# Transposing attention weights in 32x32 squares on VectorE, with a detour through DRAM, in a two-layer graph kernel

**Chip, cores, metric.** One Trainium2 chip, one core. Times are device microseconds (us) of one execution, median over runs.

## The reference

128 graphs of 128 nodes with 512 features pass through two layers. Each adds a graph operation to x and normalizes the sum. All data are fp32.

```python
def _L0_gnn_ref(x, adj, Wq, Wk, Wv):
    q = jnp.einsum('bnd,ed->bne', x, Wq); k = ...; v = ...
    rel = adj.T[None] * jnp.einsum('bnd,bmd->bnm', q, k)
    rel = rel / jnp.linalg.norm(rel, axis=2, keepdims=True)
    return jnp.einsum('bnm,bmd->bnd', rel, v)

def _L1_gnn_ref(x, adj, Wq, bq, Wk, bk, Wv, bv):        # 8 heads of 64
    q = (x @ Wq + bq).reshape(b, n, 8, 64); k = ...; v = ...
    scores = jnp.einsum('bihd,bjhd->bhij', q, k) / 8 + mask(adj)
    weights = jax.nn.softmax(scores, axis=-1)
    return jnp.einsum('bhij,bjhd->bihd', weights, v).reshape(b, n, 512)

x = _layernorm(x + _L0_gnn_ref(x, adj, ...))
x = _layernorm(x + _L1_gnn_ref(x, adj, ...))
```

## The kernel before

The 128 graphs are worked in 32 groups of four, here called batches 0 to 3. A group needs five projections of 512x512 (`m` and `v0` for layer 0; `q`, `k`, `v1` for layer 1). Each is made of seven half-sized products, in Strassen's manner, which share two PSUM banks "a" and "b" and a third, "d". Each product is 8 matmuls and takes 1.73 us from start to start.

A hand-written schedule runs in rounds of 35 slots. `dense` puts one product into a slot; `short` hangs the rest on slots, in the order in which each engine then works it off. Slot `7*j + k` belongs to projection j, so slot 21 holds the first product of the `k` projection.

```python
R = 35
for r in range(-1, NG):
    todo = [("m", r + 1), ("v0", r + 1), ("q", r), ("k", r), ("v1", r)]
    for j, (kind, g) in enumerate(todo):
        ...
        for k, i in ((0, 1), (2, 5), (3, 2), (4, 6), (5, 3), (6, 7), (8, 4)):   # slot, product
            dense[R * r + 7 * j + k] = (pr, i)
# ... layer 0, of the next group:
for b in range(G):
    at(g - 1, 10 + b, l0_score, g, b)
    at(g - 1, 18 + 2 * b, l0_out, g, b)
# ... layer 1:
    s = 31 + 5 * b
    at(g, s, attn_scores, g, b)
    at(g, s + 1, attn_max, g, b)
    at(g, s + 2, attn_exp, g, b, 0, 0)
    # ... three more pairs of exponentials
    at(g, s + 4, attn_transpose, g, b, 0)
    at(g, s + 6, attn_transpose, g, b, 1)
    at(g, s + 7, attn_out, g, b)
    at(g, s + 9, attn_stats, g, b)
    at(g, s + 11, attn_store, g, b)
```

The softmax weights are transposed by TensorE, four heads a block, and a copy brings each block from PSUM to SBUF:

```python
def attn_transpose(g, b, s):
    w, wT = SOFT[g, b][0], SOFT[g, b][3]
    wT[s] = two.tile([P, H // 2, P], F32, tag="wT", ..., bufs=3)
    p = ps_m.tile([P, H // 2, P], F32, tag="m", ...)
    for a in range(H // 2):
        nc.tensor.transpose(p[:, a, :], w[:, s, a, :], ident)
    if s: nc.scalar.copy(wT[s], p)
    else: nc.vector.tensor_copy(wT[s], p)

def attn_out(g, b):
    # ...
    for h in range(H):
        nc.tensor.matmul(p[:, h, :], wT[h % 2][:, h // 2, :], V1[g][:, b, h * HD:(h + 1) * HD], ...)
```

The layer-1 input x1 is already transposed on VectorE in 32x32 squares. DMAs inside SBUF first bring the squares to their places, 16 for each half of a group:

```python
def x1_stage(g, h):
    t = stage(g, h, "h")
    for q in range(A):
        for a in range(A):
            nc.sync.dma_start(t[q*Q:(q+1)*Q, :, a, :], X[g, h][a*Q:(a+1)*Q, :, q*P:(q+1)*P])
```

## Time and profile before

| | before |
|---|---|
| time, median of 4 runs beside the kernel after | 2782.45 us (2779.79 to 2782.64) |
| span of the profiled run, mean granted TensorE clock | 2778.2 us, 0.990 |
| busy TensorE / VectorE / ScalarE | 98% / 59% / 30% of the span |
| all DMA traffic, packet share of the queue | 143.6 MB, 19.4% |
| TensorE's waits on VectorE's copies of the weights | 3.5 us in the whole span |

TensorE is busy throughout and waits almost only at the start, so a round costs what TensorE's own instructions cost. In the profiled run I mark each round by the start of the first product of the `k` projection, slot 21 in both kernels. There are 32 marks: the first at 128.58 us, then 30 rounds of 84.15 us each, then a last round of 62.56 us (it has no `m` and `v0` work), then 62.6 us to the end.

### The profile page before, as it was taken

Reading aid. Unit: us, or ns where it says so; the run is one execution under the profiler, and the core shown is the slowest. Engines: PE = TensorE matmul, PEld = TensorE weight load, DVE = VectorE, ACT = ScalarE, POOL = GpSimd, SP = SyncE. Lnnn points to the kernel's source line nnn. Section 1 sums busy time; section 2 is a strip of 40 time slices with the busy share of each in tenths; the row PEclk is TensorE's granted clock in tenths of the full one; section 3 lists DMA queues with packets and bytes.
Section 4 is the critical chain, followed back from the end, with each engine's and each line's share of the span. In section 5 each row is a group of like instructions: output and inputs, shape, how many; then the busy total and the mean of one; then the engine's idle time right before and its main releaser. Section 6 shows DMA issues by size and latency. Waiting matters only on the chain. (4 is left out here: it accounts for less than half of the span.)

```text
span 2778.2 us, 41137 instructions
## 1 busy us (share of the span) xinstructions
PE 2726.0 (98%) x15648; PEld 2353.6 (85%) x15648; DVE 1643.9 (59%) x2709; ACT 835.5 (30%) x2951; POOL 609.5 (22%) x763
## 2 busy tenths in 40 slices
PE   7799999999999999999999999999999999999998
PEld 5688888888888888888888888888888888888877
DVE  4356656656556556566566566566566565565664
ACT  1133222332223333223333223332233322233332
POOL 4111122222122222122121222121222221222211
PEclk9899999999999999999999999999999999999998
DMA  6121121221221220222221222211212202212110
GB/s 141 46 58 43 41 57 51 57 58 29 52 58 51 56 58 27 58 55 53 58 52 33 57 53 55 58 39 45 56 51 58 58 25 56 57 51 57 42 34 21
DMA packets 193831, 143.57 MB, mean 52 GB/s; under 512 B 24928, under 2 KB 158176, under 8 KB 193632
## 3 DMA queue, kind: packets, MB, share of 16 engines
q1 hardware_dynamic: 193632, 140.94, 19.4%
q8 instruction: 123, 2.02, 0.3%
q14 instruction: 76, 0.62, 0.1%
HBM read 73.73 MB, written 33.55 MB: 39 GB/s over the span
## 5 line engine op out<-in xcount | busy, mean ns | idle before, releaser
L420 POOL TENSOR_TENSOR o<-o,x 128x512 f32<-128x512 f32 x128 | 162.2, 1267 | 1418.6 <-DVE o L418 1418.6
L394 ACT ACTIVATE w<-w,nmax 128x128 f32<-128x128 f32 x1024 | 398.8, 393 | 197.3 <-DVE nmax L388 195.7
L267 PE MATMUL pa_v<-wc_v,tx 128*128 128x256 f32 x1536 | 366.5, 381 | 0.8 <-DVE v L285 0.8
L267 PEld LDWEIGHTS pa_v<-wc_v,tx 128*128 128x128 f32 x1536 | 281.9, 190 | 38.2 <-DVE v L285 1.2
L415 PEld LDWEIGHTS po<-v,wT 128*128 128x128 f32 x2048 | 252.0, 194 | 13.0 <-DVE wT L406 4.3
L415 PE MATMUL po<-v,wT 128*128 128x64 f32 x2048 | 247.0, 274 | 5.4 <-DVE wT L406 3.5
L379 DVE SCALAR_TENSOR_TENSOR w<-ps,mask 128x1024 f32<-128x1024 f32 x128 | 156.7, 1224 | 89.3 <-PE ps L376 89.2
L267 PE MATMUL pa_m<-tx,wc_m 128*128 128x256 f32 x768 | 188.2, 388 | 21.3 <-DVE yT L285 19.1
L267 PEld LDWEIGHTS pa_q<-tx,wc_q 128*128 128x128 f32 x768 | 145.8, 190 | 59.5 <-issue 37.8
L394 ACT ACTIVATION_READ_ACCUMULATOR w<-w,nmax 128x1 f32 x1024 | 194.8, 190 | 0.0
L267 PE MATMUL pa_q<-tx,wc_q 128*128 128x256 f32 x768 | 181.5, 379 | 0.0
L267 PE MATMUL pa_k<-tx,wc_k 128*128 128x256 f32 x768 | 181.4, 379 | 0.0
L267 PEld LDWEIGHTS pa_m<-tx,wc_m 128*128 128x128 f32 x768 | 142.1, 191 | 42.7 <-issue 19.4
L418 DVE TENSOR_TENSOR o<-po,rs 128x512 f32<-128x512 f32 x128 | 88.5, 692 | 146.2 <-PE po L415 145.9
L281 ACT ACTIVATE s_q<-pa_q,bq_sb 128x256 f32<-128x256 f32 x128 | 53.6, 470 | 370.2 <-PE pa_q L267 370.2
L402 PE MATMUL pwT<-ident,w 128*128 128x128 f32 x1024 | 159.2, 277 | 4.3 <-ACT w L394 4.0
L267 PEld LDWEIGHTS pa_k<-tx,wc_k 128*128 128x128 f32 x768 | 145.9, 190 | 19.8
L376 PEld LDWEIGHTS ps<-kT,qT 64*128 64x128 f32 x2048 | 125.9, 189 | 41.5 <-issue 40.9
L402 PEld LDWEIGHTS pwT<-ident,w 128*128 128x128 f32 x1024 | 129.7, 143 | 33.1 <-ACT w L394 7.4
L388 DVE TENSOR_REDUCE nmax<-w 128x8 f32<-128x1024 f32 x128 | 154.9, 1210 | 0.0
L376 PE MATMUL ps<-kT,qT 64*128 64x128 f32 x2048 | 150.6, 287 | 0.0
L322 PE MATMUL pst<-yT,xT 128*128 128x128 f32 x1024 | 139.9, 280 | 0.0
(142 smaller groups left out, 4733.2 us busy)
## 6 DMA issues: line engine op xcount, KB each, us to landing
xl_x<-in_x_dram SPq DMA_DIRECT2D x256, 128.0 KB, 5.0
x<-in_x_dram SPq DMA_DIRECT2D x64, 512.0 KB, 5.1
xl_h<-x SPq DMA_DIRECT2D x1024, 32.0 KB, 1.9
out_dram<-o SPq DMA_DIRECT2D x128, 256.0 KB, 2.0
wv_s<-in_L_gnn_Wv_dram SPq DMA_DIRECT2D x8, 256.0 KB, 8.1
wq_s<-in_L_gnn_Wq_dram SPq DMA_DIRECT2D x1, 1024.0 KB, 5.6
wk_s<-in_L_gnn_Wk_dram SPq DMA_DIRECT2D x1, 1024.0 KB, 8.4
wq_s<-in_L_gnn_Wq_dram SPq DMA_DIRECT2D x4, 256.0 KB, 9.0
```

The source lines that it names most:

```text
L267: nc.tensor.matmul(bank[:, m, :], l[:, k, m * P:(m + 1) * P], r[:, k, :], start=start and m == 0 and k == 0, stop=(m == 1 and k == 1), ski ...
L281: nc.scalar.activation(dst[:, m], bank[:, m], AF.Identity, bias=b1[k][:, 2 * eh + m:2 * eh + m + 1])
L322: nc.tensor.matmul(p, XT[g][:, dc, b, :], YT[g][:, dc, b, :], start=(dc == 0), stop=(dc == C - 1))
L376: nc.tensor.matmul(p[:, s, a, :], QT[g][r, a, b, :], KT[g][r, a, b, :], start=True, stop=True)
L379: nc.vector.scalar_tensor_tensor(wf, p.rearrange("p s a j -> p (s a) j"), HD ** -0.5, mask[:, None, :].to_broadcast([P, H, P]), op0=ALU.mu ...
L388: nc.vector.tensor_reduce(nmax, w.rearrange("p s a j -> p (s a) j"), axis=AX.X, op=ALU.max, negate=True)
L394: nc.scalar.activation(w[:, s, a, :], w[:, s, a, :], AF.Exp, bias=nmax[:, i:i + 1], accum_out=sums[:, h:h + 1])
L402: nc.tensor.transpose(p[:, a, :], w[:, s, a, :], ident)
L415: nc.tensor.matmul(p[:, h, :], wT[h % 2][:, h // 2, :], V1[g][:, b, h * HD:(h + 1) * HD], start=True, stop=True)
L418: nc.vector.tensor_tensor(o.rearrange("p (h e) -> p h e", h=H), p, rs[:, :, None].to_broadcast([P, H, HD]), op=ALU.mult)
L420: nc.gpsimd.tensor_tensor(o, o, graph(g, b), op=ALU.add)
```

## The change

The intent is to take the 256 transpose blocks and their copies off the kernel's busiest engine. VectorE transposes only inside 32x32 squares, so the weights are written to DRAM and read back with the squares in their places. Then one VectorE instruction transposes all eight heads. x1 takes the same kind of detour in place of the 32 small copies of a group. The order of products gives VectorE more time before bank "a" is written again. `attn_out` moves from step s + 7 to s + 11. Layouts of scores, mask and maximum follow (the maximum becomes two instructions, the mask four), and the output tile `o` has two buffers in place of three.

```diff
+    def x1_spill(g, h):
+        X1D[g, h] = dram.tile([2, P, D], F32, tag="x1d", name=f"x1d_{g}_{h}")
+        nc.sync.dma_start(X1D[g, h].rearrange("b n d -> n b d"), X[g, h])
     def x1_stage(g, h):
-        t = stage(g, h, "h")
-        for q in range(A):
-            for a in range(A):
-                nc.sync.dma_start(t[q * Q:(q + 1) * Q, :, a, :], X[g, h][a * Q:(a + 1) * Q, :, q * P:(q + 1) * P])
+        load_staged(g, h, X1D.pop((g, h)))
 # ... (scores, mask, maximum and exponentials in the new layout: cut)
-    def attn_transpose(g, b, s):
-        # ... TensorE transposes and two copies, as above
+    def attn_spill(g, b, s):
+        if s == 0:
+            WD[g, b] = dram.tile([P, A, 2, H // 2 * Q], F32, tag="wd", name=f"wd_{g}_{b}")
+        nc.sync.dma_start(WD[g, b][:, :, s], SOFT[g, b][0][:, s].rearrange("p q a r -> p q (a r)"))
+    def attn_stage(g, b):
+        wl = one.tile([P, A, H, Q], F32, tag="wl", name=f"wl_{g}_{b}")
+        SOFT[g, b][0] = wl
+        rows = WD.pop((g, b)).rearrange("(a s) q t f -> s a q (t f)", s=Q)
+        for q in range(A):
+            nc.sync.dma_start(wl[q * Q:(q + 1) * Q].rearrange("p a i r -> p a (i r)"), rows[:, :, q, :])
+    def attn_transpose(g, b):
+        wT = one.tile([P, H, A, Q], F32, tag="wT", name=f"wT_{g}_{b}")
+        nc.vector.transpose(wT, SOFT[g, b][0].rearrange("p a i r -> p i a r"))
+        SOFT[g, b][0] = wT
 # ...
-            for k, i in ((0, 1), (2, 5), (3, 2), (4, 6), (5, 3), (6, 7), (8, 4)):
+            for k, i in ((0, 1), (1, 5), (3, 6), (4, 2), (5, 3), (6, 7), (9, 4)):
 # ...
-            at(g, s + 4, attn_transpose, g, b, 0)
-            at(g, s + 6, attn_transpose, g, b, 1)
-            at(g, s + 7, attn_out, g, b)
-            at(g, s + 9, attn_stats, g, b)
-            at(g, s + 11, attn_store, g, b)
+            at(g, s + 4, attn_spill, g, b, 0)
+            at(g, s + 6, attn_spill, g, b, 1)
+            at(g, s + 7, attn_stage, g, b)
+            at(g, s + 10, attn_transpose, g, b)
+            at(g, s + 11, attn_out, g, b)
+            at(g, s + 13, attn_stats, g, b)
+            at(g, s + 15, attn_store, g, b)
```

## The prediction

> **What bounds the kernel now.** I read the engine shares of the page first, then the waits of TensorE alone, then the timeline of TensorE in one steady round, then the timelines of VectorE and of the DMA queue, and last the DMA issues. The engine shares and the first waits:
>
> ```profile
> PE 2726.0 (98%) x15648; PEld 2353.6 (85%) x15648; DVE 1643.9 (59%) x2709; ACT 835.5 (30%) x2951; POOL 609.5 (22%) x763
> ...
> PE pa_m L267 <- DVE yT L285: 19.1, 1, 19.1
> PE pM L162 <- DMA wk_s<-in_L_gnn_Wk_dram: 9.7, 1, 9.7
> PE pwT L402 <- ACT w L394: 4.0, 2, 2.7
> ```
>
> TensorE works almost throughout, and all its waits together are 44 us. The longest, 19.1 us, happens once, near 79 us into the span. So a steady round costs what TensorE's instructions cost, and the other engines (DVE 59%) have room. A round of four batches takes about 84.7 us. I get this from the scores of the first batch of a group, which start at 1409.91 us and, 16 rounds later, at 2733.00 us; the last round lacks two of the five projections and the layer-0 work, some 32 us, so (1323.1 + 32) / 16 = 84.7. The cost of the transposes is read from the timeline of TensorE, by the distance between starts (columns: start, length, what):
>
> ```profile
> 1416.28 1.89 PE L267 MATMUL pa_v<-wc_v,tx 128*128 128x256 f32 x8
> 1418.01 0.60 PE L402 MATMUL pwT<-ident,w 128*128 128x128 f32 x4
> 1418.45 1.89 PE L267 MATMUL pa_m<-xT,wc_m 128*128 128x256 f32 x8
> 1420.27 1.16 PE L376 MATMUL ps<-kT,qT 64*128 64x128 f32 x16
> 1421.36 1.99 PE L267 MATMUL pa_v<-wc_v,tx 128*128 128x256 f32 x8
> 1423.19 0.60 PE L402 MATMUL pwT<-ident,w 128*128 128x128 f32 x4
> 1423.63 1.89 PE L267 MATMUL pb_m<-tx,wc_m 128*128 128x256 f32 x8
> 1425.36 1.89 PE L415 MATMUL po<-v,wT 128*128 128x64 f32 x16
> ```
>
> A block of four transposes is shown as 0.60 us long, but the next product starts 0.44 us after it. A product takes 1.73 us from start to start, whether a transpose block stands before it or not. So a block is worth 0.44 us, not 0.60.
>
> **What the Trainium skill says.** "Perfetto Trace Analysis", section "Identifying the Most-Contended Engine", warns that matmul busy time is no good measure because matmuls are pipelined. The trace agrees: the 1,024 transposes show 159.2 us busy, while 256 blocks of 0.44 us are 112.6 us. I use the second number. "VectorE: DVE Perf Modes", section "The three transpose paths", says that VectorE transposes only 32x32 blocks and does not move them across. That is why a detour is needed: the DMA must put the squares into their places. The trace has this instruction already, for x, at 699 to 702 ns for 128x512. "DMA: Bandwidth & Descriptors", section "Anatomy of one DMA", gives a fixed cost of about 2 us, mostly the receipt of the last write (stated there for transfers issued from GpSimd). The DMA issues here, from SyncE, agree in size: 2.0 us to landing for a 256 KB store. The same page, "Two DMAs through the same engine are not ordered", says that a read-back must wait for the completion of the write. So every detour pays two landings in series, and SyncE, which issues in order, stands still for the first.
>
> **Part 1, transposes off TensorE.** 256 blocks go; the 8 of the last group lie in the drain, which I count separately. 248 x 0.44 = **109 us less** on the path.
>
> **Part 2, VectorE and ScalarE.** Removed: 128 evictions of 687 ns on VectorE (88 us) and 128 of 587 ns on ScalarE (75 us). Added: 128 transposes of 128x1024. Two 128x512 sizes of about 690 ns against one 128x1024 of 1,210 ns (the maximum) put 1,024 elements at some 1.24 us, so 128 x 1.24 = 158 us. The maximum is split in two of about 0.69 us, 0.17 us more than 1.21, or 22 us. VectorE goes from 1,644 to about 1,736 us, 65% of the new span; ScalarE falls to about 760. Neither becomes the bound. The strided scores, mask and exponentials keep their element counts, hence their times.
>
> **Part 3, DMA.** Every batch writes 0.5 MB of weights in 512-byte pieces and reads them back in 1 KB pieces. That is 134 MB more, and x1's detour adds another 34 MB. How the queue behaves in the busiest stretch:
>
> ```profile
> 1449.45 0.34 SPq L432 DMA_DIRECT2D out_dram<-o  x1
> 1449.88 0.39 SPq L78 DMA_DIRECT2D x<-in_x_dram  x1
> 1450.32 5.18 SPq L90 DMA_DIRECT2D xl_x<-in_x_dram  x8
> 1455.60 0.40 SPq L78 DMA_DIRECT2D x<-in_x_dram  x1
> ```
>
> Issuing takes 0.34 to 0.65 us a piece, and the 1 MB of x in 512-byte rows passes at about 200 GB/s. Total traffic becomes about 311 MB, or 115 GB/s. The queue's share rises from 19.4% to an estimated 44%, taking 44.5 ns for a packet (19.4% of 16 x 2,778 us over 193,632 packets). It is enough, so latency decides. After the last exponential: issue 0.4, landing 2.5, four read issues 2.2, landing 2.5, in all some 8 us (my estimate from those rows). The schedule gives from step 5 after the scores to the transpose in step 10 about 10 us or more. I laid out a round of 81.2 us (84.7 less 8 x 0.44) step by step. Batches 0, 1 and 3 have 2, 6 and 4 us in hand. Batch 2 writes just before 1.5 MB of loads enter the queue (6.6 us of transfer, from the rates above). Its weights land about when VectorE asks, at 38 to 40 us against 39. I allow 0.15 us a round, **5 us more**.
>
> **Part 4, order of products.** It gives VectorE three steps instead of two between the seventh product and the fourth, which writes the same bank. That is insurance against a VectorE held up by a DMA. But the fourth product now ends directly before its first reader. In the layer-0 scores, ScalarE's copy is done about 0.2 + 0.59 us after the product, and the first half of the score (0.45 us) hides part: 0.35 us of wait. In the attention scores, two activations of 0.42 us hide less well behind a block of 1.1 us, so 0.25 us. Over 32 groups **19 us more**. Before, one product stood between and the trace shows no such wait.
>
> **Part 5, x1 and the start.** The 32 small copies become one write and four reads for each half. Before, at the start, where no layer-1 work hides it:
>
> ```profile
> 72.96 20.61 SPq L214 DMA_DIRECT2D xl_h<-x  x32
> ...
> 84.67 0.71 DVE L186 STREAM_TRANSPOSE x1T<-xl_h 128x512 f32<-128x512 f32 x1 [10.82 <-DMA xl_h<-x]
> ...
> 94.99 0.71 DVE L186 STREAM_TRANSPOSE x1T<-xl_h 128x512 f32<-128x512 f32 x1 [9.04 <-DMA xl_h<-x]
> ```
>
> The second half comes at 95 us because 32 issues take 20.6 us. In the new form: write 3.5, four issues 2.2, landing 2.5, and the same again, so about 86 us. TensorE's 19.1 us wait shrinks by **9 us**. Three more mask instructions of 0.66 us stand on VectorE's path at the start: **2 us more**.
>
> **The end.** From the last group's first scores (2733.0) to the end are 45.2 us. The new chain carries the detour, but VectorE and ScalarE of other batches overlap it. Following it batch by batch I come to about 49: **4 us more**.
>
> **Sum.** 2782.6 - 109 - 9 + 2 + 4 + 19 + 5 = 2694.6; I say 2694 us, 3.2% faster.
>
> **Rivals.** *The detour arrives late in every round.* VectorE runs in order, so a late transpose holds back the additions that free PSUM, and then TensorE. For it: the margin of batch 0 is only 2 us, and the queue blocks on each write. Against it: about 10 us of schedule against 8 of latency, and an empty queue in three of four batches. At 1.5 us a round the time is 2740; at 3 us, 2790. *TensorE loses less than it sheds.* Under the busy sum of 159 us instead of 109 the time would be about 2645; the start-to-start distances speak against it. *The new order costs nothing,* because the last product's copy hides behind the scores' own latency: then 2675. *VectorE becomes the bound:* at 65% only if its new transpose took twice my estimate; the existing ones of the same kind speak against it.
>
> **Range and chances.** Without the waits of parts 3 and 4 I get 2670; with 1.5 us a round from a late detour, 2740. The range is 2660 to 2745. The limit of 2% lies at 2728, which needs about 1 us more wait a round than I allow: I give that one chance in five.
>
> **What would show it.** TensorE's round should measure about 82 us, with waits of the layer-0 scores and of the attention scores on ScalarE of 0.2 to 0.4 us, once a round each. The new VectorE transpose should stand at 1.2 to 1.3 us, with little idle time before it except in batch 2 and at the end; the weights' write should land within 2 to 3.5 us and the reads within 2 to 5. VectorE should be near 65% and the DMA share near 44%. The prediction is wrong if the transposes wait for the DMA in most batches and TensorE then waits for VectorE, or if the products of a round no longer start 1.73 us apart.

## The result, and the profile after

The kernel after takes **2795.23 us** (median of 4 runs, 2794.52 to 2798.01) against 2782.45 us: a ratio of 1.005 (95% interval 1.0033 to 1.0067), that is, the same within 2%. Ratios here are the mean time of one kernel's fast runs over the mean of the other's of the same rounds, so not quite the ratio of the medians. The prediction was 2694 us.

The engine shares of the page after, then the groups of the new DMA transfers (columns: number, KB each, us from issue to landing) and the group of the new transpose:

```profile
PE 2677.6 (96%) x14624; PEld 2282.5 (82%) x14624; DVE 1690.0 (61%) x2840; ACT 770.9 (28%) x2823; POOL 598.8 (21%) x761
...
wd<-w SPq DMA_DIRECT2D x256, 256.0 KB, 2.4
wl<-wd SPq DMA_DIRECT2D x512, 128.0 KB, 2.8
```

```profile
L416 DVE STREAM_TRANSPOSE wT<-wl 128x1024 f32<-128x1024 f32 x128 | 158.3, 1237 | 2.9 <-DMA wl<-wd 2.9
```

The durations in the prediction held: 1,237 ns for the new transpose, 2.4 us to land a write, 2.8 us a read, VectorE at 61% (I said 65%), the DMA queue at 37.7% (I said 44%). VectorE waited for the weights' DMA for 2.9 us in the *whole* span. So the detour itself is in time. Yet TensorE waits for that transpose once in nearly every round. Two lines of the waits of TensorE (us in total, times, longest):

```profile
PE po L426 <- DVE wT L416: 59.6, 34, 5.2
...
PE pst L323 <- ACT yT L276: 7.4, 32, 0.2
```

The first is the wait that I had dismissed. The second I had predicted, from the new order: the layer-0 score directly after the product that it reads. Here it is in the timeline of TensorE:

```profile
1437.86 0.61 PE L323 MATMUL pst<-yT,xT 128*128 128x128 f32 x4
1438.69 0.71 PE L323 MATMUL pst<-yT,xT 128*128 128x128 f32 x4 [0.23 <-ACT yT L276]
1439.24 1.89 PE L268 MATMUL pa_v<-wc_v,tx 128*128 128x256 f32 x8
```

The idle time shown is not the whole price: from start to start this score takes 1.38 us here, and 0.89 in e3 below, where nothing holds it up.

The other wait, for batch 3's weights, in the same timeline:

```profile
1466.66 1.89 PE L268 MATMUL pa_q<-tx,wc_q 128*128 128x256 f32 x8
1468.39 1.89 PE L268 MATMUL pa_k<-x1T,wc_k 128*128 128x256 f32 x8
1471.73 2.00 PE L426 MATMUL po<-v,wT 128*128 128x64 f32 x16 [1.46 <-DVE wT L416]
1473.57 1.08 PE L360 MATMUL po<-v,rel 128*128 128x512 f32 x2
```

From `pa_k` to `po` is 3.34 us, where a product takes 1.73. What was VectorE doing? SyncE's issues of the four reads of batch 3, and then VectorE's timeline up to the transpose:

```profile
1460.01 1.74 SPq L412 DMA_DIRECT2D wl<-wd  x4
```

```profile
1466.60 0.69 DVE L193 TENSOR_TENSOR tx<-xT 128x512 f32<-128x512 f32 x1
...
1467.81 0.74 DVE L362 SCALAR_TENSOR_TENSOR x<-po,rn,x 128x512 f32<-128x512 f32 x1
1468.59 0.69 DVE L342 BATCH_NORM_STATS2 bs<-x 128x6 f32<-128x512 f32 x1
...
1469.41 0.66 DVE L286 TENSOR_TENSOR qT<-pa_q,s_q 128x512 f32<-128x512 f32 x1
1469.99 0.54 DVE L354 TENSOR_SCALAR o<-o,st,rstd 128x512 f32<-128x512 f32 x1
1470.44 1.24 DVE L416 STREAM_TRANSPOSE wT<-wl 128x1024 f32<-128x1024 f32 x1
```

The last issue ends at 1461.75, and the trace has the last of the four reads landing at 1464.18. The transpose starts at 1470.44, six microseconds later, without a wait of its own: in the order in which VectorE works off its instructions here, others stand before it. How full VectorE is there, from the windows view, with the transpose itself and then from the landing to its start (us, then busy time and instructions of PE, PEld, DVE, ACT, POOL; clock; DMA share; GB/s):

```profile
1459.90:1471.60 11.70, 10.38 (x44) 8.04 (x43) 10.05 (x17) 1.68 (x4) 2.06 (x3) 1.00 0.16 51
...
1464.18:1470.44 6.26, 6.10 (x27) 4.65 (x25) 6.09 (x12) 0.07 (x1) 0.79 (x2) 1.00 0.00 0
```

VectorE is busy 10.05 of 11.70 us, 86%, in the wider stretch, and 97% from the landing on, against 61% on average: results of layer 0 with their statistics, transposes of the next x, and additions of the `q` projection all meet there.

There is a second loss. The mean granted clock fell from 0.990 to 0.975. In some rounds the matmuls *behind* the wait run at half speed for 3.4 us. A round of that kind, in TensorE's timeline and in the windows view:

```profile
458.39 2.00 PE L426 MATMUL po<-v,wT 128*128 128x64 f32 x16 [1.45 <-DVE wT L416]
460.23 1.73 PE L360 MATMUL po<-v,rel 128*128 128x512 f32 x2
461.75 2.98 PE L268 MATMUL pb_k<-tx,wc_k 128*128 128x256 f32 x8
```

```profile
460.50:464.00 3.50, 3.50 (x8) 2.14 (x7) 2.56 (x5) 0.00 (x0) 1.27 (x1) 0.51 0.00 0
```

The clock is 0.51 in that window, and the layer-0 product `po<-v,rel` is shown as 1.73 us in place of 1.08. Rounds without such a spell measure 83.18 us, rounds with it 84.86, so a spell costs 1.68 us. 21 of the 30 full rounds have one.

By marks, the spans compare so (us):

| stretch | before | after | difference |
|---|---|---|---|
| to the first mark | 128.58 | 122.42 | -6.2 |
| 30 rounds, mean | 84.15 | 84.25 | +2.9 in all |
| last round | 62.56 | 67.41 | +4.9 |
| from the last mark to the end | 62.6 | 75.7 | +13.1 |

The sum is +14.7, the difference of the spans (2792.9 - 2778.2).

### The profile page after: what moved, and what is told of

The parts are those of the page before. It is cut to its first block, busy times and chain, and to the rows that moved or that the text cites. A ratio compares the mean times of both kernels' runs of the same rounds, so it can differ in the third digit from the quotient of the medians.

```text
span 2792.9 us, 39712 instructions
## 1 busy us (share of the span) xinstructions
PE 2677.6 (96%) x14624; PEld 2282.5 (82%) x14624; DVE 1690.0 (61%) x2840; ACT 770.9 (28%) x2823; POOL 598.8 (21%) x761
## 3 DMA queue, kind: packets, MB, share of 16 engines
q1 hardware_dynamic: 407648, 308.71, 37.7%
## 5 line engine op out<-in xcount | busy, mean ns | idle before, releaser
L426 PEld LDWEIGHTS po<-v,wT 128*128 128x128 f32 x2048 | 258.2, 200 | 91.2 <-DVE wT L416 72.6
L426 PE MATMUL po<-v,wT 128*128 128x64 f32 x2048 | 259.8, 282 | 72.4 <-DVE wT L416 59.6
L389 DVE TENSOR_REDUCE nmax<-w 128x4 f32<-128x512 f32 x256 | 162.7, 677 | 1.1
L377 PE MATMUL ps<-kT,qT 64*128 64x128 f32 x2048 | 161.2, 293 | 0.0
L416 DVE STREAM_TRANSPOSE wT<-wl 128x1024 f32<-128x1024 f32 x128 | 158.3, 1237 | 2.9 <-DMA wl<-wd 2.9
L362 DVE SCALAR_TENSOR_TENSOR x<-po,rn,x 128x512 f32<-128x512 f32 x128 | 95.7, 748 | 104.5 <-PE po L360 63.9
L323 PE MATMUL pst<-yT,xT 128*128 128x128 f32 x1024 | 148.2, 283 | 7.4 <-ACT yT L276 7.4
L360 PE MATMUL po<-v,rel 128*128 128x512 f32 x256 | 150.2, 672 | 2.6 <-DVE x L362 1.9
```

The lines of the kernel that those rows point to most:

```text
L323: nc.tensor.matmul(p, XT[g][:, dc, b, :], YT[g][:, dc, b, :], start=(dc == 0), stop=(dc == C - 1))
L360: nc.tensor.matmul(p, REL[g][0][:, b, :], V0[g][:, b, :], start=True, stop=True)
L362: nc.vector.scalar_tensor_tensor(h, p, RN[g][:, b:b + 1], h, op0=ALU.mult, op1=ALU.add)
L377: nc.tensor.matmul(p[:, s, :, a, :], QT[g][r, a, b, :], KT[g][r, a, b, :], start=True, stop=True)
L389: nc.vector.tensor_reduce(nmax[:, s * (H // 2):(s + 1) * (H // 2)], w[:, s].rearrange("p q a r -> p a q r"), axis=AX.XY, op=ALU.max, negat ...
L416: nc.vector.transpose(wT, SOFT[g, b][0].rearrange("p a i r -> p i a r"))
```

## The experiments

**Theory Q (queue).** Batch 3's transpose is late because it stands behind other work in VectorE's own order, which fills 97% of the time since the weights landed; the pause in turn trips TensorE's clock. **Rival D (detour).** The weights arrive late from DRAM. **Rival C (clock by itself).** The half clock comes from the doubled DMA traffic, or from elsewhere, not from the pause. **Rival B (busy sum).** The removed transposes were never worth 3.5 us a round.

All kernels below gave correct results. "Round" is the distance of marks in the profiled run. e1 to e4 ran on one chip, e5 to e8 on a second and e9 to e11 on a third, each set beside runs of the kernel before on its own chip; those had medians of 2782.2, 2783.0 and 2782.8 us, so the sets can be compared. e1 to e7 and e11 have four runs each.

### e1: batch 3's transpose one step earlier

```diff
-            at(g, s + 10, attn_transpose, g, b)
+            at(g, s + (9 if b == 3 else 10), attn_transpose, g, b)
```

> The changed kernel, with the weights' transpose of batch 3 alone one step earlier in VectorE's order (step 9 after its scores, not 10). Theory 1, VectorE's queue: the weights have landed near 3 us before they are transposed, but two layer-0 evictions with their statistics stand ahead; moved ahead of them, the transpose ends before TensorE asks, the wait of 1.45 us a round goes, the half-clock spells that follow it go too, and the time falls from 2795 to about 2712 (30 rounds x (1.7 + 1.25) us less, some 88, a few us either way). Rival 2, late detour: VectorE then idles for the DMA at the transpose in each round and the time stays above 2780. Rival 3, half clock from another cause (the DMA traffic): the wait goes, the half-clock spells stay, about 2745.

Measured: **2707.44 us**, ratio 0.9735 [0.9721, 0.975]. The round is 81.46 us in 29 of 30 cases (the first, 79.72, lacks batch 3's output of a group before); the wait and all half-clock spells in the steady rounds are gone. TensorE's timeline at the same place:

```profile
1425.99 1.89 PE L268 MATMUL pa_k<-x1T,wc_k 128*128 128x256 f32 x8
1427.72 1.89 PE L426 MATMUL po<-v,wT 128*128 128x64 f32 x16
```

Had the weights been late, VectorE would now stand and wait for them. Its waits for them in the whole span:

```profile
DVE wT L416 <- DMA wl<-wd: 3.4, 4, 1.9
```

That is 3.4 us against 2.9. Rival D falls: one line in a schedule, with the same DMAs, is worth 88 us. Rival C falls as far as DMA traffic goes: the traffic is the same and the spells are gone. The wait alone is 83.18 - 81.46 = 1.72 us a round.

### e2: batch 3's output one step later

```diff
-            at(g, s + 11, attn_out, g, b)
-            at(g, s + 13, attn_stats, g, b)
-            at(g, s + 15, attn_store, g, b)
+            l = 1 if b == 3 else 0
+            at(g, s + 11 + l, attn_out, g, b)
+            at(g, s + 13 + l, attn_stats, g, b)
+            at(g, s + 15 + l, attn_store, g, b)
```

> The changed kernel, with the use of batch 3's transposed weights (and its statistics and store) one step later; VectorE's order of the transpose is untouched. Theory 1: TensorE has another product to do while the transpose is still in the queue; wait and half clock go, about 2712 us, as in the first run. Rival 2 (late detour) also gives a gain here, since the use comes later, so only the two runs together tell them apart. Rival 3: about 2745.

Measured: **2709.6 us**, ratio 0.974 [0.9725, 0.9754], round 81.46. Moving the reader back does what moving the transpose forward does. This run alone would not tell Q from D, since both gain from a later reader; with e1 it shows that one slot of slack suffices on either side.

### e3: the change with the old order of products

```diff
-            for k, i in ((0, 1), (1, 5), (3, 6), (4, 2), (5, 3), (6, 7), (9, 4)):
+            for k, i in ((0, 1), (2, 5), (3, 2), (4, 6), (5, 3), (6, 7), (8, 4)):
```

> The changed kernel with the old order of the seven products. Theory: the short waits of the layer-0 scores (0.48 us a round from start to start) and of the first attention scores (0.33 us) go, 0.8 us a round, while the wait of batch 3 and the half clock stay: about 2770 us. Rival: the new order is needed, the fourth product waits for VectorE's addition in some round and the time is 2795 or more.

Measured: **2715.85 us**, ratio 0.9765 [0.975, 0.9779], some 54 us better than I expected. The wait did not stay at 1.46 us. TensorE's timeline:

```profile
1428.25 1.89 PE L268 MATMUL pa_k<-x1T,wc_k 128*128 128x256 f32 x8
1430.85 2.00 PE L426 MATMUL po<-v,wT 128*128 128x64 f32 x16 [0.70 <-DVE wT L416]
```

It fell to 0.70 us, and with that no steady round has a half-clock spell: 28 of the 30 measure 81.61 us (the first 78.85, one 81.97). My expectation had treated order and wait as independent. They are not. The new order puts product 2, and so its addition, one step later. VectorE's timeline shows what follows, first in e3 and then in the kernel after:

```profile
1421.63 0.69 DVE L286 TENSOR_TENSOR qT<-pd_q,s_q 128x512 f32<-128x512 f32 x1 [0.54 <-PE pd_q L268]
1422.48 0.75 DVE L362 SCALAR_TENSOR_TENSOR x<-po,rn,x 128x512 f32<-128x512 f32 x1 [0.16 <-PE po L360]
```

```profile
1462.62 0.75 DVE L362 SCALAR_TENSOR_TENSOR x<-po,rn,x 128x512 f32<-128x512 f32 x1 [1.40 <-POOL o L431]
...
1464.35 0.69 DVE L286 TENSOR_TENSOR qT<-pd_q,s_q 128x512 f32<-128x512 f32 x1
```

In both kernels VectorE has the same 16 instructions from batch 2's output to the transpose, 8.9 us of work. In e3 it does the addition of product 2 (`qT<-pd_q`) before the layer-0 result and idles 0.9 us in all; in the kernel after it idles 1.6, of which 1.40 before the layer-0 result, and has the addition still to do. (The view names GpSimd there, but that instruction had ended at 1461.95; TensorE's product for this result ends at 1462.51.) The idle time comes close to the 0.76 us by which the wait is longer; no run moved this one addition alone. The order that was to insure against a late VectorE made VectorE late.

### e4: early transpose and old order together

The edits of e1 and e3 together.

> Both: batch 3's transpose one step earlier and the old order of products. If the two costs add up: 2795 - 88 - 24 = about 2685 us. If the old order exposes VectorE's delays (rival): no better than the first run alone, about 2712.

Measured: **2682.63 us**, ratio 0.9644 [0.9628, 0.966], against 2685 expected. The round is 80.64 us in 29 of 30 cases (the first is 78.85), 3.51 below the kernel before: exactly the eight transpose blocks at 0.44 us. Rival B falls in its strong form (5.0 us a round from the busy sum of 159 us). The new order's price without the other losses is e1 minus e4: 81.46 - 80.64 = 0.82 us a round.

### e5: the kernel before with the new order only

The edit is e3's, reversed, on the kernel before.

> The kernel before with the new order of the seven products alone. If the order costs what it cost between the runs e1 and e4 (0.83 us a round), and nothing hides it: 2782 + 26 = 2808 us. But here a block of transposes (0.44 us) stands between the fourth product and the first layer-0 score and should hide most of that wait, so 0.33 to 0.4 us a round and about 2794 us. Rival: the order costs nothing by itself and only its meeting with the late transpose did: 2782 us.

Measured: **2799.47 us**, ratio 1.0063 [1.0048, 1.0078]. The round is 84.70 us, 0.55 more than before where I had expected 0.33 to 0.4, and the last round is longer by 4.35 us, at a mean clock of 0.90 against 0.95 in the same stretch before. So the new order costs by itself; it needs no detour to do so. The cost is under 2%, but clear of the noise. That the last round suffers more than the others I had not foreseen.

### e6: the kernel before with x1's detour only

```diff
+    def x1_spill(g, h): ...          # as in the change
     def x1_stage(g, h):
+        load_staged(g, h, X1D.pop((g, h)))
-            at(g - 1, 28 + 2 * h, x1_stage, g, h)
+            at(g - 1, 28 + 2 * h, x1_spill, g, h)
+            at(g - 1, 29 + 2 * h, x1_stage, g, h)
```

> The kernel before with x1's detour through DRAM alone. Theory: the steady round stays at 84.15 us, only the start gains, since x1's second half lands some 6 to 9 us sooner; the time falls by 6 to 9 us to about 2775. Rival: the write to DRAM and its wait hold the queue up in every round and the time is 2785 or more.

Measured: **2771.1 us**, ratio 0.9963 [0.9946, 0.9979]. The round is unchanged at 84.15. The first mark comes 7.8 us earlier: TensorE's longest wait shrinks from 19.1 to 11.0 us. x1's detour pays once, at the start, where nothing hides it.

### e8, e9, e10: a pause put into the kernel before

To test the clock by itself, the kernel before gets a pause of TensorE at the comparable place, before batch 3's output: ScalarE repeats its copy of the weights n times. There is no DRAM detour of the weights and no new order.

```diff
         if s:
+            for _ in range(n if b == 3 else 0):      # e9: 3, e8: 4, e10: 6
+                nc.scalar.copy(wT[s], p)
             nc.scalar.copy(wT[s], p)
```

> The kernel before with four idle repeats of ScalarE's copy ahead of the last half of batch 3's transposed weights (the same data again, the result unchanged): a pause of TensorE of about 1.3 us once a round at the same place as in the changed kernel, with no detour and no added DMA. Theory: the pause by itself drops the clock: half-clock spells of 3.4 us in many rounds, and a round of 84.15 + 1.4 + about 1.2 us. Rival (the DMA traffic or VectorE's transposes drop the clock): the round grows by the pause alone, and the clock stays full.

> As the run with four repeats, with three: a pause of about 1.05 us. In that run a pause of 1.54 us halved the clock in every third round, and the starts of its spells lie whole multiples of 3.413 us apart. Theory: a pause counts by how much of one such window it empties, so a shorter one falls below the limit in every position: no spells, a round of about 85.3 us, some 2818 us in all. Rival: any pause at this place can trip it when the position is right, and some rounds still show spells.

> The same with six repeats: a pause of about 2.5 us. Theory: a longer pause empties enough of a window in more positions, so spells come in more than one round in three, in half of them or more; a round of about 86.9 us without a spell and 1.7 us more with one. Rival: the share of rounds with a spell stays at one in three.

Each is one run, so I read the rounds within one profile and not the times: e9 **2818.56**, e8 **2856.37**, e10 **2933.98 us**. Two neighbouring rounds of e8 in TensorE's timeline, both with a pause of 1.54 us, the first without and the second with a spell:

```profile
1416.25 1.77 PE L417 MATMUL po<-v,wT 128*128 128x64 f32 x14 [1.54 <-ACT wT L406]
1417.87 1.08 PE L359 MATMUL po<-v,rel 128*128 128x512 f32 x2
1418.78 1.89 PE L267 MATMUL pa_q<-tx,wc_q 128*128 128x256 f32 x8
...
1502.15 1.77 PE L417 MATMUL po<-v,wT 128*128 128x64 f32 x14 [1.54 <-ACT wT L406]
1503.76 1.69 PE L359 MATMUL po<-v,rel 128*128 128x512 f32 x2
1505.25 3.01 PE L267 MATMUL pa_q<-tx,wc_q 128*128 128x256 f32 x8
```

| kernel | pause a round | round without / with a spell | rounds with a spell |
|---|---|---|---|
| e3 | 0.70 us | 81.61 / - | none |
| e9 | 0.93 us | 85.29 / - | none |
| after | 1.46 us | 83.18 / 84.86 | 21 of 30 |
| e8 | 1.54 us | 85.90 / 87.59 | 10 of 30, every third |
| e10 | 2.8 us | 87.14 / 88.83 (some 90.48) | 28 of 30 |

The pauses came out at 0.93, 1.54 and 2.8 us, where 1.05, 1.3 and 2.5 were expected; the theories on how often spells come held in all three.

A kernel with the old traffic gets the same spells, at the same price (87.59 - 85.90 = 1.69 us), by a pause alone. Together with e1 this settles it: the pause trips the clock. Why do equal pauses trip it in some rounds only? The spells are 3.413 us long (some in e10 twice that), and from the start of one to the next there are whole multiples of 3.413 us (mostly 26 in e10; 76 in e8; 25 or 49 after). So the decision falls in windows that run freely beside the program, and whether a pause of 1.5 us counts depends on where it lies in one. The traces of the kernel after bear this out. If windows of 3.413 us are laid through the starts of the spells, of the 29 pauses in the steady rounds the 21 that begin between 0.37 us before a window's start and 0.83 us after it bring a spell, which starts with the next window; the 8 that begin 0.44 to 0.83 us before a window's start bring none.

Which share of a window must be idle stays open. The idle time alone does not decide: in e8, pauses with 1.3 us at the end of a window brought no spell, while in the kernel after 1.1 us at the start of one did. What the thin matmuls behind the pause (64 columns) contribute, no run tested.

### e7: e4, with the last two groups in the old way

The drain after the last mark is 75.7 us in the kernel after and 73.6 in e4, against 62.6 before. e7 keeps the functions of both kernels; the groups 30 and 31 use TensorE's transposes.

```diff
+            if g >= NG - 2:
+                at(g, s, pe_attn_scores, g, b)
+                # ... the schedule and functions of the kernel before
+                continue
```

> The run e4 with the last two groups by the old way (TensorE's transposes, the old steps), 30 groups by the detour. In these two groups TensorE has little other work, so the detour's latency stands open: in e4 the last round takes 65.95 us and the drain from its mark to the end 68.4, against 61.7 and 59.1 before. If the detour is the cause, both return to the old values: 2682 - 4 - 9 + 3.5 (one group's transposes back in a full round) = about 2672 us. Rival: the drain is long for another reason (the clock is at half there in both), and the time stays at 2682 or rises.

Measured: **2675.98 us**, ratio 0.9618 [0.9604, 0.9632]. The drain is back at 62.4 us, so its lengthening was the detour's. The last round fell by 0.4 us to 66.39, much as the expected -4 and +3.5 would have it. The first mark, though, came at 128.09 in place of 122.94 us: this kernel needs the old mask as well as the new one, five instructions on VectorE's path at the start. (The marks in the expectations of e7 and e11 are those of the second product of `k`, some 4 us later; the values here are by the marks of the rest of this document.)

### e11: e7, with the masks made at an idle point

```diff
-    nc.vector.tensor_scalar(mask_p, adj_sb, 0.0, NEG, ...)      # and four for the new mask
+    def masks(): ...                                             # the same five instructions
+    at(-1, 14, masks)
```

> The hybrid of run e7 with the five mask instructions moved out of the start, to a point where VectorE is idle (nothing else changed). In the start of e7 the first products wait for VectorE's additions behind these instructions, and its first mark lies at 132.4 us against 127.3 in e4, which has one mask instruction less. If they are the cause, some 3 to 8 us come off: 2668 to 2673 us. Rival: the start is bound by x1's detour and by the weights of layer 1, and the time stays at 2676.

Measured: **2666.54 us**, ratio 0.9586 [0.957, 0.9602]; first mark 118.45, round 80.64, drain 62.4. Of the gain over e7, 9.6 us lie before the first mark, where the masks were, and 2.0 in the last round (64.36 us), which has one half-clock window of 3.4 us less. It is the fastest version here, 4.1% faster than the kernel before. Engine shares of its page:

```profile
PE 2620.6 (98%) x14688; PEld 2259.8 (85%) x14688; DVE 1682.8 (63%) x2833; ACT 775.4 (29%) x2831; POOL 591.5 (22%) x763
```

TensorE is back at 98%, which says that the freed time is no longer lost in waits.

## Why the prediction was wrong

Step by step, in the prediction's own terms (us over the whole run):

| step | predicted | shown |
|---|---|---|
| part 1, transposes off TensorE | -109 | 3.51 a round (before - e4), over 30 rounds -105 |
| part 3, batch 3's wait | +5 for waits on a late detour | 1.72 a round (after - e1), +52, with no late detour |
| half clock after that wait | not foreseen | 21 spells of 1.68, +35 |
| part 4, new order | +19, 0.6 a round | 0.82 a round (e1 - e4), +25 |
| part 5, start | -7 | -6.2 |
| the end | +4 | last round +4.9, drain +13.1 |

(The first interval after the first mark is 3.45 us shorter in the kernel after, 79.73 us: batch 3's output, with its wait, now lies just behind the mark. With this the first four rows, unrounded, give +2.8 for the 30 rounds, where the marks show +2.9.)

**Right:** reading a block's worth from start to start (0.44 us) and not from its shown length; the duration of the new transpose; the latency and the capacity of the DMA; the gain at the start; and the kind of wait that the new order brings. From start to start the layer-0 scores lose about 0.5 us, where I had worked out 0.35, and the first attention scores 0.33 (1.42 in place of 1.09), where I had 0.25. Two readings were off without harm: a round before is 84.15 us and not 84.7, because the last round is 23 us shorter than the others and not 32 (by the scores' marks), and 1.5 MB at the 200 GB/s shown take about 7.5 us, not 6.6. And the trace agrees with the cited warning about busy time, not with the page's reason, as the closing list says.

**The step that failed** is in part 3: "It is enough, so latency decides", with "Batches 0, 1 and 3 have 2, 6 and 4 us in hand". I counted the reserve from the landing of the weights to the slot of the transpose, as if VectorE were free in that slot. The weights of batch 3 landed 4.7 to 6.3 us before the transpose in the steady rounds, even earlier than I had said (batches 0 and 1 had mostly 2.7 and 5.7 us, batch 2 about 0.1 to 1.3, much as predicted); but VectorE took the transpose up late, and TensorE waited 1.46 us. The rival "*VectorE becomes the bound*" I dismissed "at 65%", an average, where VectorE was at 97% from the landing of the weights to this transpose. Of the signs of being wrong that I had named, the first, transposes that wait for the DMA, did not come. And in part 4 I called the new order "insurance against a VectorE held up by a DMA", priced only its effect on TensorE, and never asked what it would do to VectorE's order: it doubled the wait (e3: 0.70 us in place of 1.46).

**The rival that came closest** was the first, "*The detour arrives late in every round*": its arithmetic ("at 3 us, 2790") fits the result, for wait and half clock together are 2.9 us a round. But its mechanism is wrong, as e1 shows; had one believed it, one would have added buffers or moved the DMAs, though batch 3's weights already lay ready for 6 us (no run tried it).

**The term that was missing** is the clock. I took a wait to cost its own length. Here 1.7 us of wait brought on average 1.2 us more.

**The end** I had put at +4. The drain alone took 13.1 us more, and e7 shows that the detour causes it. The profile has TensorE waiting 3.4 to 5.9 us a batch there and 38.6 us at half clock, against 24.0 before. How much of it is the wait and how much the clock was not separated. The last round of the kernel after has 17.1 us at half clock, against 6.8 before. In e11, with the old way there, it is back at 6.8, and the round is only 1.8 us longer than before, about what batch 3's output, which now lies behind the mark, takes (1.73). So the detour lengthens the last round too; e7, with one half-clock window more and 66.39 us, shows that the clock has a share in it.

## What to carry to other kernels

Where a change gives an in-order engine a new hand-over to the bound engine, look at its queue in the very stretch before the hand-over, not at its share of the span: one slot more of reserve, in the transpose or in its reader, was worth 88 us here. Test each part of a change alone; the order of products that came along as insurance cost time in both kernels and made the wait longer. A pause of TensorE of some 1.5 us can cost twice, by itself and by the clock behind it, so look at the granted clock around every recurring wait.

## What the Trainium skill lacked or had wrong

- "TensorE: Matmul & The Clock Gate", section "HAM oscillation — how this bites in real kernels", gives as its rule no idle gaps of TensorE above some 3.4 us (its next section, on a second failure mode, says that frequent micro-idles can do it too, without a length). Here pauses of 1.46 and 1.54 us halved the clock in part of the rounds (21 of 30, and every third) and 2.8 us in 28 of 30; 0.70 and 0.93 us did in none. The rule allows too much, for recurring gaps at least. The page's section "What's actually happening" speaks of a free-running window of about 3.4 us, and that agrees: spells of 3.413 us, whole multiples of it apart.
- "VectorE: DVE Perf Modes", section "The three transpose paths", times only a bf16 block of 128x128 and calls its 32x32 squares "Useful for some layouts, useless for others". In fp32, 128x1024 took 1,237 ns in one instruction, and with a DRAM detour that is scheduled well (e4) this saved TensorE 3.51 us a round. No page gives what a block of four fp32 transposes costs amid other matmuls: it was shown as 0.60 us and worth 0.44.
- "Perfetto Trace Analysis", section "Identifying the Most-Contended Engine", gives as its reason that pipelined PE instructions look smaller in the trace. Here the transposes looked larger: 159.2 us busy, worth 112.6 from start to start.
- No page that I read warns that an engine which is never the most contended can still be full just before a hand-over, and that its average share hides this: 61% over the span, 97% in the 6.3 us that decided.
